# Attention products of two local-attention models: the order of row halves in two of them, and which operand is loaded in a third

## Chip, cores and metric

The kernel runs on one core of a Trainium2 chip. The metric is the device time of one execution in microseconds (us). The kernel before was run three times: 4997.42, 5001.14 and 5006.03 us, median 5001.14.

## What is computed

The input is x with 2 x 2048 rows of 128 features, all in float32. Four blocks follow each other, each behind a layer norm with a modulation and with a gated residual:

1. an attention in chunks of 64 rows with a running memory,
2. the **first model**: six layers of local attention (16 heads of 64, windows of 32 rows) and feed-forward,
3. a causal linear attention with feed-forward,
4. the **second model**: two layers of local attention (8 heads of 64, windows of 64 rows) and feed-forward.

The change touches only the local attention of the two models. Cut to what matters, one layer of it is:

```python
qkv = shift(x) @ Wqkv                      # W = 32, 16 heads; or W = 64, 8 heads
q, k, v = heads(qkv)                       # heads of 64 features
q, k = rotary(l2norm(q) * qs, l2norm(k) * ks)
# each window of W rows sees its own W keys and those of the window before
sim = einsum('bhwie,bhwje->bhwij', q * 8.0, look(k))     # 2W keys per row
sim = where(mask, -max, sim)
attn = softmax(sim)
out = einsum('bhwij,bhwje->bhwie', attn, look(v))
x = x + merge_heads(out) @ Wo
x = x + feed_forward(shift(x))
```

## The kernel before

The function `local_models` runs both models and the linear attention between them as one stream of tiles. A tile is 128 rows of one batch. A layer has 32 tiles (16 in each of two batches), so there are 6 x 32 = 192 tiles of the first model and 2 x 32 = 64 of the second. The main loop (line 1471) is a software pipeline: in one turn it works on the scores of tile i+1, on the projection of queries and keys of tile i+3 (`project`), on the values of tile i+2 (`values`), on the value product and the output of tile i (`mix`, `turn_out`, `project_out`). The work of the feed-forward and of the linear attention is put in between in steps. The order in which the program is written gives priorities; a planner then sets the final order of the instructions on each engine and gives out the buffers. [...] The activations lie with features on the partitions (`hs`), so that a tile of them can be the loaded operand of the projections.

The steps of a tile that matter here:

- `scores` (line 974): a mask is put into two banks of PSUM by two products (line 986), and the products of queries and keys are added to it. `q` counts the two halves of the rows of the operands: partitions 0 to 63 hold one head and partitions 64 to 127 another, since a head has 64 features. `w` counts the windows in a tile, NW = 4 in the first model and 2 in the second. `cc` counts pairs of heads, 8 and 4. So there are 64 products a tile in the first model (64 rows deep, 32 columns loaded, 64 moving) and 16 in the second (64 deep, 64 loaded, 128 moving). A product's output goes to the partitions of its window; its half q decides the bank.
- softmax over the scores: VectorE takes the maximum and subtracts it (1003, 1005), ScalarE the exponential (1012), VectorE the sums (1019), GpSimd the scaling (1021).
- `keys_first_` (line 1023): TensorE turns the weights so that the keys lie on the partitions, and ScalarE copies them into `pT` (1031), which has one buffer, shared with `oT`.
- `mix` (line 1034): the value product. `NO` is 2 in the first model and 1 in the second: 2W keys fill 64 or 128 partitions, so that in the first model the two halves `s` of the rows hold different heads, whose outputs go to two banks `po[s]`. In the first model there are 64 products of 64 x 32 loaded by 64 moving, in the second 16 of 128 x 64 by 64. The turned weights `pT` are loaded, the values `v2` move; the result has the tile's rows on the partitions. ScalarE copies it into `on` (1053).
- `turn_out` (line 1056): TensorE turns `on` (4 transposes for each of NO), ScalarE copies it into `oT` (1064).
- `turn` (line 923): TensorE turns queries and keys of tile i+2 (936).
- `project_out` (line 1067): the product of the output weights with `oT` (1075), added to the residual by VectorE (1081).

The profile counts each float32 product as two records, and each transpose as one.

Of the kernel before, what the change touches and what calls it, by code (L numbers as in the profile page):

```python
# [72 lines left out]
def tile_kernel(ctx: ExitStack, tc: tile.TileContext, a: dict, out: bass.AP):  # L73
    nc = tc.nc
# [26 lines left out]
    def bc(ap, shape):  # L101
        return ap.to_broadcast(list(shape))
# [605 lines left out]
    def local_models(mA, mB, hs0):  # L708
# [8 lines left out]
        def wide(name):  # L717

            return psA.tile([128, 1024], F32, tag="A", name=f"ps_{name}")

        def bank(name):
            return psT.tile([128, 512], F32, tag="T", name=f"ps_{name}")
# [53 lines left out]
        st = [dict() for _ in range(n)]  # L776
# [4 lines left out]
        def load_proj(g, u):  # L781

            m, l = layers[g]
            w = wpool.tile([128, 1024], F32, tag="wp", name="wp", bufs=4)
            c = u * 1024
            k = min(1024, 3 * m.INNER - c)
            nc.sync.dma_start(w[:, 0:k], a[f"{m.pre}_ffn_Wqkv"][l, :, c:c + k])
            wts[g, u] = w

        def load_out(g):  # L790
            m, l = layers[g]
            w = wpool.tile([128, 8, 128], F32, tag="wo", name="wo", bufs=2)
            nc.sync.dma_start(
                w[:, 0:m.NPR, :], a[f"{m.pre}_ffn_Wo"][l].rearrange("(c p) m -> p c m", p=128)
            )
            wts[g, "o"] = w
# [41 lines left out]
        def factors(g):  # L838
            m, l = layers[g]
            f = wk.tile([128, 2, 2, DH], F32, name="fac", bufs=2)  # L840
            nc.vector.scalar_tensor_tensor(
                f[:, 0], m.sc, RSQ_C, m.qsc[:, :, l, :], ALU.mult, ALU.mult
            )
            for lo in (0, 32):
                nc.vector.tensor_copy(f[:, 1, :, lo:lo + 32], f[:, 0, :, 32 - lo:64 - lo])
            fac[g] = f
# [127 lines left out]
        def scores(i):  # L974

            g, b, t = tiles[i]
            m, _ = layers[g]
            W, H, HPG = m.W, m.H, m.HPG
            qT, kT = st[i].pop("q"), st[i].pop("k")
            sp = wide("s")  # L980
            for q in range(2):


                rows, sel, j = (slice(0, 128), identb, 0) if t == 0 else (
                    slice(64 * q, 64 * q + 64), pick, 1)
                nc.tensor.matmul(
                    sp[:, 512 * q:512 * q + 512], lhsT=sel[rows],
                    rhs=bc(m.maskb[rows, j].unsqueeze(1), (rows.stop - rows.start, HPG, 2 * W)),
                    start=True, stop=False,
                )  # L990
            for cc in range(HPG):
                for q in range(2):
                    for w in range(m.NW):
                        c0 = 512 * q + 2 * W * cc
                        nc.tensor.matmul(  # L995
                            sp[W * w:W * w + W, c0:c0 + 2 * W],
                            lhsT=qT[64 * q:64 * q + 64, cc, W * w:W * w + W],
                            rhs=kT[64 * q:64 * q + 64, cc, W * w:W * w + 2 * W],
                            start=False, stop=(cc == HPG - 1),
                        )  # L1000
            v = lambda x: x.rearrange("p (h k) -> p h k", k=2 * W)
            mx = wk.tile([128, 16], F32, name="mx")
            nc.vector.tensor_reduce(mx[:, 0:H], v(sp), AX.X, ALU.max)  # L1003
            sm = wk.tile([128, 1024], F32, name="sm", bufs=2)
            nc.vector.tensor_tensor(
                v(sm), v(sp), bc(mx[:, 0:H].unsqueeze(2), (128, H, 2 * W)), ALU.subtract
            )
            st[i]["p"] = sm

        def weights_exp(i):  # L1010
            sm = st[i]["p"]
            nc.scalar.activation(sm, sm, AF.Exp)  # L1012

        def weights_norm(i):
            m, _ = layers[tiles[i][0]]
            sm = st[i]["p"]
            v = sm.rearrange("p (h k) -> p h k", k=2 * m.W)
            rs = wk.tile([128, 16], F32, name="rs", bufs=2)[:, 0:m.H]
            nc.vector.tensor_reduce(rs, v, AX.X, ALU.add)  # L1019
            nc.vector.reciprocal(rs, rs)  # L1020
            nc.gpsimd.tensor_tensor(v, v, bc(rs.unsqueeze(2), (128, m.H, 2 * m.W)), ALU.mult)  # L1021
# [12 lines left out]
        def mix(i):  # L1034

            m, _ = layers[tiles[i][0]]
            W, NO = m.W, m.NO
            pT, v2 = st[i].pop("pT"), st[i].pop("v")
            po = [bank("o") for _ in range(NO)]
            on = wk.tile([128, 2, 4, 128], F32, name="on")  # L1040
            for c in range(4):
                for s in range(NO):
                    kp = slice(2 * W * s, 2 * W * (s + 1))
                    for q in range(2):
                        co = 128 * c + 64 * q
                        for w in range(m.NW):
                            nc.tensor.matmul(  # L1047
                                po[s][W * w:W * w + W, co:co + 64],
                                lhsT=pT[kp, q, c, W * w:W * w + W],
                                rhs=v2[kp, w, co:co + 64], start=True, stop=True,  # L1050
                            )
            for s in range(NO):
                nc.scalar.copy(on[:, s].rearrange("p c i -> p (c i)"), po[s])  # L1053
            st[i]["on"] = on
# [34 lines left out]
        def step():  # L1089
            if steps:  # L1090
                steps.pop(0)()
# [4 lines left out]
        def lstep():  # L1096
            if lsteps:
                lsteps.pop(0)()
# [372 lines left out]
        for i in range(-3, n):  # L1471
            j = i + 3
            lstep()
            if 0 <= i + 1 < n:
                scores(i + 1)
                weights_exp(i + 1)
                weights_norm(i + 1)
            more = False
            if j < n:
                g, b, t = tiles[j]  # L1480
                jj = j % per
                nu = len(layers[g][0].units)
                more = g < last
                if g == second and t % 4 == 0:
                    while (b, t // 4) not in ready:
                        lstep()
                if nu == 2:
                    project(j, 0)
                if more and jj == 4:
                    load_proj(g + 1, 0)  # L1490
                if more and jj == 6 and g + 1 == second:
                    models[1].consts()
                if jj == 6 and g == second - 1:
                    linear_consts()
                if more and jj == 8:
                    factors(g + 1)
                    if 2 == 2:
                        load_out(g + 1)
                if more and jj == 18:
                    load_ff(g + 1)  # L1500
                if more and jj == 22:
                    fold_ff(g + 1)
                if nu == 2 and more and jj == per - 1:
                    load_proj(g + 1, 1)
                lstep()
            step()
            if i >= 0:
                keys_first_(i)
            if 0 <= i + 2 < n:
                halo(i + 2)  # L1510
            if j < n:
                project(j, nu - 1)
                if nu == 2 and more and jj == per - 1 and g + 1 < second:
                    load_proj(g + 1, 2)
                if nu == 1 and more and jj == per - 1:
                    load_proj(g + 1, 1)
                if b == B - 1 and j + 1 < n:
                    tables(*tiles[j + 1][::2])
            lstep()
            if i >= 0:  # L1520
                mix(i)
            lstep()
            if 0 <= i + 2 < n:
                values(i + 2)
            lstep()
            if i >= 0:
                turn_out(i)
            if 0 <= i + 2 < n:
                for u in range(len(layers[tiles[i + 2][0]][0].units)):
                    turn(i + 2, u)  # L1530
            step()
            lstep()
            if i >= 0:
                g, b, t = tiles[i]
                project_out(i)
                if 2 == 1 and i % per == per - 1 and g < last:
                    load_out(g + 1)
                if t % 4 == 3:
                    feed_forward(g, b, t // 4)
# [9 lines left out]
    with ExitStack() as ctx2:  # L1549
        local_models(m0, m1, hs0)  # L1550
# [63 lines left out]
```

## Time and profile before

| | |
|---|---|
| runs, median | 5001.14 us |
| profiled execution, own time | 5004.26 us |
| its span | 5002.5 us |
| granted TensorE clock, mean | 0.961 |
| TensorE, matmuls busy | 4572.7 us (91%) |
| TensorE, weight loads busy | 3143.2 us (63%) |
| VectorE busy | 3973.1 us (79%) |
| ScalarE busy | 2883.5 us (58%) |
| GpSimd busy | 2780.8 us (56%) |
| chain of waits | TensorE 53%, VectorE 20%, ScalarE 8%, GpSimd 5% |

The span divides into the first block, up to about 641 us, the first model, from there to about 4050 us (with the first steps of the linear attention in its last layer), and the second model, to the end. Busy time is the time in which at least one instruction of the group was under way, so that overlapping records count once; it is smaller than the count times the mean. A line of a group reads: line, engine, operation, output and inputs by name, shapes and count, then busy us and mean ns of one, then the idle time of the engine just before these instructions and what ended most of it. For TensorE, 64\*32 is the loaded operand's depth and columns, and 64x64 the moving operand.

### The profile page before, as it was taken

The numbers are of one execution on the slowest core, as the hardware profiler recorded it, in microseconds if no ns is written. First come the engines' busy times: TensorE is split into PE (matmuls) and PEld (weight loads), VectorE is DVE, ScalarE is ACT, GpSimd is POOL, SyncE is SP. The second block draws the span as 40 slices with busy tenths as digits, with TensorE's granted clock in tenths as the row PEclk, the third lists the DMA queues.
The fourth block names the chain that finished last, engine by engine and source line by source line (L and its number), as shares of the span: only waits on it lengthen the run. The fifth ranks groups of instructions, "written<-read, shape, count | busy, mean of one in ns | idle before, by whom it ended". The sixth has DMA issues, their size and how long they took to land.

```text
span 5002.5 us, 170719 instructions
## 1 busy us (share of the span) xinstructions
PE 4572.7 (91%) x74820; PEld 3143.2 (63%) x74850; DVE 3973.1 (79%) x6840; ACT 2883.5 (58%) x4665; POOL 2780.8 (56%) x1666
## 2 busy tenths in 40 slices
PE   5667799999999999999999999999999989899897
PEld 4445566666666666666666666666666666555554
DVE  6993488888888888888888888888877777787885
ACT  3233366666666656666666666666555555565564
POOL 3332366666666666666666666666555544455452
PEclk8778899999999999999999999999999999999999
DMA  2000322222222322223222322232222211111111
GB/s 77 1 1 25 84 69 67 63 72 74 71 64 63 83 71 63 63 76 76 66 66 64 83 67 64 65 78 73 54 55 52 63 45 38 39 46 40 53 53 37
DMA packets 222487, 295.59 MB, mean 59 GB/s; under 512 B 75656, under 2 KB 95408, under 8 KB 221744
## 3 DMA queue, kind: packets, MB, share of 16 engines
q1 hardware_dynamic: 221744, 284.67, 22.0%
q8 instruction: 590, 9.67, 0.8%
q14 instruction: 153, 1.25, 0.1%
HBM read 40.98 MB, written 10.75 MB: 10 GB/s over the span
## 4 chain that ended last, share of the span: by engine, by line
PE 53%; DVE 20%; ACT 8%; POOL 5%; issue 3%; DMA 1%; SPq 0%; POOLq 0%; ACTq 0%; DVEq 0%
PE ps_qk L871 11%; PE ps_v L955 6%; PE ps_f L1158 5%; PE ps_turn L936 5%; PE ps_y L1075 5%; PE ps_o L1047 5%; PE ps_s L995 4%; DVE ps_qk L897 4%; POOL r L892 3%; DVE t L886 3%; PE ps_fy L1183 3%; PE ps_oT L1063 3%; ACT sq L873 2%; DVE r L881 2%; PE ps_pT L1030 2%
## 5 line engine op out<-in xcount | busy, mean ns | idle before, releaser
L892 POOL TENSOR_TENSOR r<-r,t 128x1024 f32<-128x1024 f32 x448 | 1061.2, 2369 | 995.9 <-DVE t L886 770.5
L904 POOL TENSOR_TENSOR r<-r,rq_y 128x1024 f32<-128x1024 f32 x448 | 844.0, 1902 | 455.9 <-DVE rq_y L180 439.2
L873 ACT ACTIVATE sq<-ps_qk 128x1024 f32<-128x1024 f32 x448 | 460.4, 1028 | 1006.4 <-PE ps_qk L871 999.9
L871 PE MATMUL ps_qk<-wp,hs 128*128 128x512 f32 x1792 | 884.4, 615 | 68.3 <-DVE rq_y L180 41.3
L881 DVE TENSOR_TENSOR r<-ps_qk,tb 128x1024 f32<-128x1024 f32 (+1 forms) x512 | 550.1, 1074 | 175.4 <-ACT sq L873 166.9
L886 DVE TENSOR_TENSOR t<-ps_qk,tb 128x1024 f32<-128x1024 f32 (+1 forms) x512 | 553.2, 1080 | 145.0 <-POOL r L892 144.5
L1021 POOL TENSOR_TENSOR sm<-sm,rs 128x1024 f32<-128x1024 f32 x256 | 487.2, 1903 | 263.3 <-DVE rs L1020 172.3
L897 DVE TENSOR_REDUCE ps_qk<-sq 128x16 f32<-128x1024 f32 x448 | 549.1, 1226 | 12.3
L1047 PEld LDWEIGHTS ps_o<-v,pT 64*32 64x32 f32 (+1 forms) x26624 | 356.8, 109 | 289.1 <-ACT pT L1031 175.7
L871 PEld LDWEIGHTS ps_qk<-wp,hs 128*128 128x128 f32 x1792 | 306.7, 191 | 326.2 <-issue 235.6
L955 PE MATMUL ps_v<-wp,hs 128*128 128x512 f32 x896 | 471.9, 639 | 1.0 <-ACT on L1053 0.6
L1047 PE MATMUL ps_o<-v,pT 64*32 64x64 f32 (+1 forms) x26624 | 418.1, 224 | 59.6 <-ACT pT L1031 32.7
L1075 PEld LDWEIGHTS ps_y<-oT,wo 128*128 128x128 f32 x3584 | 429.2, 192 | 48.0 <-issue 42.2
L936 PE MATMUL ps_turn<-ident,r 128*128 128x128 f32 x3584 | 443.2, 276 | 13.3 <-POOL r L904 11.8
L1075 PE MATMUL ps_y<-oT,wo 128*128 128x128 f32 x3584 | 446.3, 276 | 1.8 <-ACT oT L1064 1.8
L936 PEld LDWEIGHTS ps_turn<-ident,r 128*128 128x128 f32 x3584 | 405.7, 143 | 19.8 <-POOL r L904 16.6
L1003 DVE TENSOR_REDUCE mx<-ps_s 128x16 f32<-128x1024 f32 (+1 forms) x256 | 312.9, 1222 | 110.8 <-PE ps_s L995 107.4
L995 PE MATMUL ps_s<-kT,qT 64*32 64x64 f32 (+1 forms) x26624 | 371.6, 230 | 0.4
L1019 DVE TENSOR_REDUCE rs<-sm 128x16 f32<-128x1024 f32 (+1 forms) x256 | 310.3, 1212 | 68.6 <-ACT sm L1012 67.5
L1158 PE MATMUL ps_f<-fx,w 128*128 128x512 f32 (+1 forms) x768 | 356.4, 600 | 1.7 <-DVE fx L1141 1.7
L995 PEld LDWEIGHTS ps_s<-kT,qT 64*32 64x32 f32 (+1 forms) x26624 | 321.3, 107 | 57.1 <-issue 46.2
L956 ACT COPY vn<-ps_v 128x512 f32<-128x512 f32 x448 | 262.5, 586 | 112.3 <-PE ps_v L955 93.4
(268 smaller groups left out, 7554.6 us busy)
## 6 DMA issues: line engine op xcount, KB each, us to landing
v<-vn SPq DMA_DIRECT2D x1276, 128.0 KB
v<-vn SPq DMA_DIRECT2D x744, 64.0 KB
v<-vn SPq DMA_DIRECT2D x64, 256.0 KB
wp<-in_L_ffn_Wqkv SPq DMA_DIRECT2D x20, 512.0 KB
xD<-xb SPq DMA_DIRECT2D x24, 256.0 KB
xb<-xD SPq DMA_DIRECT2D x24, 256.0 KB
cs<-in_cos SPq DMA_DIRECT2D x128, 32.0 KB
cs<-in_sin SPq DMA_DIRECT2D x128, 32.0 KB
```

The costliest lines, as they stand in the source:

```text
L871: nc.tensor.matmul(pq[:, js], lhsT=hw, rhs=wts[g, u][:, js], start=True, stop=True)
L881: nc.vector.tensor_tensor(r[:, es].rearrange("p (h d) -> p h d", d=DH), pq[:, es].rearrange("p (h d) -> p h d", d=DH), bc(tb[:, 0, s].unsq ...
L886: nc.vector.tensor_tensor(t2[:, es].rearrange("p (h s d) -> p h s d", s=2, d=32), pq[:, es].rearrange("p (h s d) -> p h s d", s=2, d=32)[: ...
L892: nc.gpsimd.tensor_tensor(r, r, t2, ALU.add)
L897: nc.vector.tensor_reduce(pq[:, 16 * v:16 * v + 16], st[i].pop(("sq", v)).rearrange("p (h d) -> p h d", d=DH), AX.X, ALU.add,)
L904: nc.gpsimd.tensor_tensor(rv, rv, bc(y[:, 16 * v:16 * v + 16].unsqueeze(2), (128, 16, DH)), ALU.mult)
L936: nc.tensor.transpose(p[:, c * 128:(c + 1) * 128], r[:, cs], ident)
L955: nc.tensor.matmul(p, lhsT=hw, rhs=wv, start=True, stop=True)
L995: nc.tensor.matmul(sp[W * w:W * w + W, c0:c0 + 2 * W], lhsT=qT[64 * q:64 * q + 64, cc, W * w:W * w + W], rhs=kT[64 * q:64 * q + 64, cc, W ...
L1047: nc.tensor.matmul(po[s][W * w:W * w + W, co:co + 64], lhsT=pT[kp, q, c, W * w:W * w + W], rhs=v2[kp, w, co:co + 64], start=True, stop=True,)
L1075: nc.tensor.matmul(py[:, 0:128], lhsT=wts[g, "o"][:, c * NO + s, :], rhs=oT[:, s, c, :], start=(c + s == 0), stop=(c == 3 and s == NO - 1),)
L1158: nc.tensor.matmul(ps_[c][0:sz], lhsT=wts[g, "w1"][:, o:o + sz], rhs=S["x"], start=True, stop=True,)
```

## The change

There are three edits.

1. In `scores` the loops over w and q change places: the products go from one half of the rows to the other at each product, where before one half had NW products in a row. This applies to both models.
2. In `mix` for the first model the loop over s goes from second to innermost: the two halves s alternate at each product, where before one half had eight products in a row.
3. In `mix` for the second model the operands change places: `v2` is the loaded operand and `pT` moves. The result has the features on the partitions, as `project_out` needs it, so it is copied once into `on` and goes to `project_out` from there. `turn_out` is left out for tiles of the second model.

```diff
             for cc in range(HPG):
-                for q in range(2):
-                    for w in range(m.NW):
+                for w in range(m.NW):
+                    for q in range(2):
                         c0 = 512 * q + 2 * W * cc
...
             on = wk.tile([128, 2, 4, 128], F32, name="on")
+            if NO == 1:
+
+                for c in range(4):
+                    for w in range(m.NW):
+                        for q in range(2):
+                            co = 128 * c + 64 * q
+                            nc.tensor.matmul(
+                                po[0][64 * q:64 * q + 64, 128 * c + W * w:128 * c + W * w + W],
+                                lhsT=v2[:, w, co:co + 64], rhs=pT[:, q, c, W * w:W * w + W],
+                                start=True, stop=True,
+                            )
+                nc.scalar.copy(on[:, 0].rearrange("p c i -> p (c i)"), po[0])
+                st[i]["o"] = on
+                return
             for c in range(4):
-                for s in range(NO):
-                    kp = slice(2 * W * s, 2 * W * (s + 1))
-                    for q in range(2):
-                        co = 128 * c + 64 * q
-                        for w in range(m.NW):
+                for q in range(2):
+                    co = 128 * c + 64 * q
+                    for w in range(m.NW):
+                        for s in range(NO):
+                            kp = slice(2 * W * s, 2 * W * (s + 1))
                             nc.tensor.matmul(
...
-            if i >= 0:
+            if i >= 0 and "on" in st[i]:
                 turn_out(i)
```

## The prediction

> **What bounds the kernel now.** I read the table of stretches first, then the groups by shape of TensorE, then single blocks in the timeline, and last the waits of the second model.
>
> Columns of the first fence: the stretch, then busy time (and records) of PE, PEld, DVE, ACT and POOL, the granted clock, DMA share, GB/s. The first row is one layer of the first model, 32 tiles; the second is most of the second model.
>
> ```profile
> 1735.00:2289.00 554.00, 539.03 (x10430) 374.47 (x10432) 463.34 (x741) 349.08 (x560) 354.25 (x206) 0.99 0.28 69
> 4562.00:5002.00 440.00, 380.89 (x3324) 242.25 (x3320) 331.38 (x679) 243.81 (x368) 196.94 (x121) 0.96 0.17 46
> ```
>
> In a layer of the first model TensorE is busy 539 of 554 us, VectorE 463 (84%). A microsecond taken from TensorE there comes off the end nearly whole, until VectorE is next. In the second model TensorE has 381 of 440 (87%), VectorE 75%: no engine is full, and waits count too.
>
> ```profile
> L1047 PE MATMUL ps_o<-v,pT 64*32 64x64 f32 x24448 | 324.5, 223 | 36.2 <-issue 26.0 <-ACT pT L1031 9.2
> L995 PE MATMUL ps_s<-kT,qT 64*32 64x64 f32 x24192 | 292.3, 225 | 0.4
> ...
> L1063 PE MATMUL ps_oT<-ident,on 128*128 128x128 f32 x1532 | 201.7, 275 | 2.3 <-ACT on L1053 2.3
> ```
>
> These are the first model (641 to 4050 us). The two small-product groups have the same 64 products (128 records) for each of 192 tiles. Per tile the scores take 292.3/192 = 1.52 us and the value product 324.5/192 = 1.69 us: 0.17 us more for the same count of the same size.
>
> The stretches inside one scores block (first two rows, line L995) and one value block (last two, L1047) show where. Every window is 0.24 us long; a record counts if it overlaps the window.
>
> ```profile
> 2256.87:2257.11 0.24, 0.24 (x32) 0.24 (x33) 1.00 0.28 68
> 2257.80:2258.04 0.24, 0.24 (x44) 0.24 (x27) 1.00 0.86 188
> ...
> 2316.24:2316.48 0.24, 0.24 (x25) 0.24 (x29) 1.00 0.00 0
> 2317.20:2317.44 0.24, 0.24 (x44) 0.24 (x35) 1.00 0.00 0
> ```
>
> The first window starts with nothing in flight: scores 32 records in 0.24 us, 7.5 ns each; values 25, 9.6 ns each. Later records last some 0.22 us, so 44 overlapping ones mean 44/(0.24+0.22) = 96 a microsecond, 10.5 ns each, the same in both. So the blocks differ in their opening, where work stands ready; afterwards both go at one pace, which I read as the pace of issue.
>
> In the second model:
>
> ```profile
> L1063 PE MATMUL ps_oT<-ident,on 128*128 128x128 f32 x252 | 42.4, 293 | 27.8 <-ACT on L1053 27.3
> L1064 ACT COPY oT<-ps_oT 128x512 f32<-128x512 f32 x63 | 37.0, 588 | 36.8 <-PE ps_oT L1063 36.8
> L1053 ACT COPY on<-ps_o 128x512 f32<-128x512 f32 x63 | 36.7, 582 | 25.9 <-PE ps_o L1047 25.7
> ```
>
> The turning of the output costs TensorE 42.4 us busy and 27.8 us idle, waiting for the copy of `on`. One tile of it, in the timeline of TensorE:
>
> ```profile
> 4588.18 1.04 PE L1047 MATMUL ps_o<-v,pT 128*64 128x64 f32 x28
> 4589.90 0.66 PE L1063 MATMUL ps_oT<-ident,on 128*128 128x128 f32 x4 [0.68 <-ACT on L1053]
> 4590.39 1.04 PE L936 MATMUL ps_turn<-ident,r 128*128 128x128 f32 x8
> ```
>
> The value product is over, TensorE stands 0.68 us, and the turns of `r` that are queued behind stand too.
>
> [...]
>
> **The change part by part.**
>
> *Scores, 192 tiles (and 64 of the second model).* Same instructions; TensorE's order outside the block is the same in the first model but for its first steady tile. The old order runs four products on one row half, then four on the other, so all eight tiles of the array come round once in eight products; the new order also visits each once in eight. As nothing in the opening or the pace of issue should change, I take 0. Bounds: if everything ran at the opening's 7.5 ns, a block would take 128 x 7.5 ns + 0.23 us = 1.19 us, 0.33 less, 63 us in all; a loss is treated as a rival. In the second model the order goes from row half outermost to strip outermost over four tiles, whose 32 records take 1.10 us: 0.
>
> *First model's value product, 192 tiles.* Here the old order has eight products in a row on one row half: each of the four tiles gets two products before the other half is touched. Alternating gives it the scores' pattern, so I expect the scores' time at best: 0.17 x 192 = 32 us. Part of the 0.17 is not order: in some tiles the block is cut by a value projection (L955) and pays its tail, one record of 0.22 us, and a restart a second time. Such cuts number some 40 by the timeline; at about 0.3 us they make 12 us. So 20 us, bounds 0 and 0.50 x 192 = 96 us (1.69 to 1.19). All on the path, TensorE being 97% busy.
>
> *Second model's value product, 64 tiles.* 16 products with the 64 columns of V as loaded operand and 64 token columns moving; before 64 token columns loaded and 64 of V moving. Shape 128x64 by 128x64 either way, the two column strips alternate either way: 0. The result already has the features on the partitions.
>
> *Removed: turning the output, 64 tiles.* Four transposes and one ScalarE copy a tile: on TensorE 42.4 us busy, and up to 27.8 us of standing. On ScalarE 37.0 us, which is busy 244 of 440 us there and so has room: 0 by themselves. The lower bound is the 2.8% that the chain of waits from 4050 to 5002 us gives to `ps_oT`: 0.028 x 952 = 27 us. The upper is 42.4 + 27.8 = 70 us. TensorE is busy 87% here, and part of the standing will come back as waits for VectorE, whose max and subtraction have 4.6% and 4.9% of that chain. I take 48.
>
> *What is late next.* `project_out` now waits for the copy of `on` itself. Between the value product and it, TensorE has the eight turns of `r` (1.04 us) and mostly a value projection (1.13 us); the copy takes 0.58 us. Covered; without cover it would be 0.6 x 64 = 38 us. Behind that wait stand the next tile's mask and score products. The single buffer of `on` is now held until `project_out` has read it, which precedes the next value product on TensorE: no wait. The buffer shared by `pT` and `oT` is freed after the value product instead of after `project_out`: the copy of the next `pT` can go earlier, which I leave at 0, as it is queued on ScalarE behind others.
>
> *The planner's order in the second model* changes on all engines: VectorE and GpSimd swap neighbours (scaling of `r` and of `sm`), and SP issues its fetches and stores of x in other places among the value copies. SP's DMA share there is 0.17, so these stay hidden. I take 0, between -15 and +15 us.
>
> *Sum.* 20 + 48 = 68 us. The profiled execution ran 5004.26 us (span 5002.5 and 1.8 around it), so 4936; the median of the runs shown, 5001.14, is 3 lower. 4935 allows for part of that.
>
> **Rivals.**
> 1. *Alternation speeds the whole block* (both blocks at 7.5 ns throughout): 63 + 96 + 48 = 207 us, about 4795. For it: the opening shows that the array can. Against: the scores already change halves every four products and yet fall to 10.5 ns. Chance 0.08.
> 2. *The turning was in the shadow*: the freed 42.4 us of the second model are eaten by VectorE's chain (subtraction and max lead it), less than 15 remain: 5001 - 20 - 10 = about 4971 to 4981. For it: 13% idle on TensorE. Against: TensorE itself stood for 27.8 us there. Chance 0.13.
> 3. *Slower: two halves in one column strip exclude each other.* In the new order neighbours sit in the same strip. The opening's eight tiles at 7.5 ns mean about 8 x 7.5 = 60 ns for one record on its tile; if only four strips work, 128/4 x 60 ns + 0.23 = 2.15 us a block, +0.63 for scores and +0.46 for values, 209 us in all, less 48: about 5160; half of it, about 5060. It decides from 48/192 = 0.25 us per tile. Against it stands the first stage, whose scores already alternate halves in one strip:
>
> ```profile
> 445.58 1.09 PE L411 MATMUL ps_s<-kx,qT 64*64 64x512 f32 x8
> ```
>
> Eight records of 512 columns in 1.09 us, while two such full-height records of `ps_v` alone take 1.13: the four tiles run together. Chance 0.07.
>
> That the change doesn't do what it says is out: four transposes a tile are gone from TensorE's order.
>
> **How the numbers follow.** Main case 0.72, at 4935; its own range is 4880 to 4968 (20 may be 0 to 60, 48 is 27 to 70). With the second rival the range becomes 4882 to 4983 and leaves out the first and third, 0.15. A measurement here tells 0.2%, 10 us, from no change. Faster by more than that: 0.72 + 0.08 + nearly all of 0.13, 0.91; within: 0.02; slower: 0.07.
>
> **What would show it.** L995 64*32 near 292 us and the value product's row near 305; no `ps_oT` rows after 4050 and no idle time of `ps_y` for the copy of `on`; a layer of the first model 3 us shorter, the second model some 45. Wrong if score blocks change by more than 0.1 us either way, or if the second model keeps its length.

## The result: slower by half a per cent, and the profile after

Five runs of the changed kernel and five of the kernel before on the same chip gave medians of 5023.68 us (5021.63 to 5036.48) and 5006.03 us (4997.42 to 5007.68). The ratio is 1.0047, with a 95% interval from 1.0033 to 1.0061: slower by 17 to 31 us. The forecast was 66 us faster. The profiled execution took 5036.48 us (span 5034.7), the longest of the five.

From the first residual addition of each layer (L1081 before, L1095 after) the time divides so:

| us | before | after |
|---|---|---|
| to the first residual of the first model | 641.5 | 649.2 |
| first model, six layers | 3408.9 | 3432.1 |
| second model, to the end | 952.0 | 953.4 |

The first row holds nothing that was changed, and in the profiles below it lies between 635 and 650 us, so that two single profiles can differ by 7 us a stage, or some more, without cause. The first model lost 23 us, and the second gained nothing. Both gains of the forecast are missing, so there are two questions.

The stretches that the prediction began with, in the changed kernel (its first row lies some 17 us earlier in the work):

```profile
1735.00:2289.00 554.00, 534.24 (x10430) 369.52 (x10430) 463.55 (x744) 348.46 (x561) 354.00 (x207) 0.99 0.28 69
4562.00:5002.00 440.00, 380.98 (x3413) 246.17 (x3412) 340.19 (x711) 230.07 (x347) 217.66 (x133) 0.95 0.17 48
```

TensorE is busy 534 us where it was 539, for the same number of records: it has less to do in a layer, and takes as long. In the second model it is busy 381 of 440 us, as before.

**First model.** The two groups, in the groups by shape of TensorE over the first model of the changed kernel. L1061 is the value product, L1047 before.

```profile
L1061 PE MATMUL ps_o<-v,pT 64*32 64x64 f32 x24448 | 306.9, 226 | 64.4 <-issue 53.1 <-ACT pT L1031 10.3
L995 PE MATMUL ps_s<-kT,qT 64*32 64x64 f32 x24384 | 294.3, 226 | 0.7 <-issue 0.5
```

The busy time did what was forecast: 306.9 us where 305 was written, and the scores are at 12.1 ns a record as before (294.3/24384; 292.3/24192). In the blocks without a gap the 32nd record starts 0.26 us after the first (0.33 before) and the 128th 1.27 us (1.36 before), in the middle of all such blocks: most of the gain lies in the opening, as was argued. The last part of the row is what matters. TensorE stands 64.4 us ahead of records of this group (36.2 before), and 53.1 us of it (26.0 before) carry the name "issue", for which the profile shows no releaser. A busy row that falls by 17.6 us beside an idle entry that grows by 28.2 us is a loss, though only of 11 of the 23 us.

One tile shows where. This is TensorE's timeline around the value product of the fifteenth tile, first of the kernel before, then of the changed one (start, length, line, records, and in brackets the idle time ahead).

```profile
861.96 1.02 PE L871 MATMUL ps_qk<-wp,hs 128*128 128x512 f32 x2
862.92 1.80 PE L1047 MATMUL ps_o<-v,pT 64*32 64x64 f32 x128
864.65 1.12 PE L955 MATMUL ps_v<-wp,hs 128*128 128x512 f32 x2
```

```profile
872.92 1.50 PE L1061 MATMUL ps_o<-v,pT 64*32 64x64 f32 x107
876.51 0.42 PE L1061 MATMUL ps_o<-v,pT 64*32 64x64 f32 x21 [2.09 <-issue]
876.86 0.70 PE L955 MATMUL ps_v<-wp,hs 128*128 128x512 f32 x1
```

After 107 of its 128 records the block stands for 2.09 us, though all of its operands were there: the 21 records behind the gap use the same `pT` and `v2`. The stretches of 0.5 us in the same tile (busy time and records of PE, granted clock, DMA share, GB/s) show what happens meanwhile:

```profile
872.92:873.42 0.50, 0.46 (x30) 1.00 0.00 0
873.42:873.92 0.50, 0.50 (x64) 1.00 0.16 33
873.92:874.42 0.50, 0.50 (x54) 1.00 0.00 0
874.42:874.92 0.50, 0.00 (x1) 1.00 0.00 0
...
876.42:876.92 0.50, 0.41 (x22) 1.00 0.00 0
```

33 GB/s over 0.5 us are 16 KB: one transfer, in the middle of the block. It belongs to the queue that the page calls instruction:

```profile
q8 instruction: 588, 9.63, 0.8%
```

9.63 MB in 588 packets are 16 KB each. TensorE's part of this trace has 150632 records, counting matmuls, weight loads and the semaphore instructions of its queue: 256 for each packet. So I counted these records through the trace. Every one of the changed kernel's 35 gaps of over 0.6 us inside a value block lies at the same place of the count, 163 modulo 256 give or take one, and so do all 16 of the kernel before. (Without the semaphore instructions the places scatter.) In each of the 35 the first record behind the gap follows 1.2 to 1.6 us after the end of the transfer of a packet. From this I read the gap as TensorE waiting for its next packet of instructions. These gaps make 28.5 us before and 60.7 us after. In the fifteenth tile, counted from the previous edge:

| us after the previous edge | before | after |
|---|---|---|
| next packet begins | 0.86 | 5.79 |
| value block begins | 4.83 | 4.84 |
| block reaches the packet's end | 6.17 | 6.12 |
| first record of the next packet | 6.18 | 8.42 |

After, the first record of the next packet follows 2.63 us behind the packet's beginning. Before, the packet began at once and had 5.3 us; after, it began 4.9 us later, only when the block was already running.

**Second model.** First the turning of queries and keys in the groups of the kernel before from 4050 to 5002 us, then the groups of the changed kernel from 4081 to 5034 us. L1089 is `project_out`, L1172 the hidden layer of the feed-forward (L1158 before).

```profile
L936 PE MATMUL ps_turn<-ident,r 128*128 128x128 f32 x488 | 67.8, 285 | 8.3 <-POOL r L904 8.3
```

```profile
L936 PE MATMUL ps_turn<-ident,r 128*128 128x128 f32 x488 | 73.8, 297 | 32.8 <-POOL r L904 32.8
L1089 PE MATMUL ps_y<-on,wo 128*128 128x128 f32 x507 | 72.8, 290 | 1.5 <-ACT on L1052 1.5
L1172 PE MATMUL ps_f<-fx,w 128*128 128x512 f32 x144 | 81.4, 693 | 2.1 <-DVE fx L1155 1.8
```

No row of `ps_oT` is left, and `project_out` waits 1.5 us in all for the copy of `on`: that cover held. But the turning of `r` (L936) now waits 32.8 us for GpSimd's scaling of `r` (L904), 8.3 before.

### The profile page after: what moved, and what is told of

Read it like the earlier page. It is cut to its first block, busy times and chain, and to the rows that moved or that the text cites. A ratio compares the mean times of both kernels' runs of the same rounds, so it can differ in the third digit from the quotient of the medians.

```text
span 5034.7 us, 170087 instructions
## 1 busy us (share of the span) xinstructions
PE 4557.0 (91%) x74564; PEld 3122.2 (62%) x74594; DVE 3968.2 (79%) x6840; ACT 2840.4 (56%) x4591; POOL 2784.4 (55%) x1666
## 3 DMA queue, kind: packets, MB, share of 16 engines
q8 instruction: 588, 9.63, 0.8%
## 4 chain that ended last, share of the span: by engine, by line
PE 54%; DVE 19%; ACT 7%; POOL 5%; issue 3%; DMA 1%; SPq 0%; POOLq 0%; DVEq 0%; ACTq 0%
PE ps_qk L871 12%; PE ps_v L955 6%; PE ps_turn L936 5%; PE ps_f L1172 5%; PE ps_y L1089 5%; PE ps_s L995 4%; PE ps_o L1061 4%; DVE ps_qk L897 4%; DVE t L886 4%; POOL r L892 3%; PE ps_fy L1197 3%; DVE r L881 2%; PE ps_oT L1077 2%; PE ps_pT L1030 2%; ACT sq L873 2%
## 5 line engine op out<-in xcount | busy, mean ns | idle before, releaser
L904 POOL TENSOR_TENSOR r<-r,rq_y 128x1024 f32<-128x1024 f32 x448 | 844.6, 1903 | 443.6 <-DVE rq_y L180 427.0
L936 PE MATMUL ps_turn<-ident,r 128*128 128x128 f32 x3584 | 451.1, 278 | 41.3 <-POOL r L904 36.3
L936 PEld LDWEIGHTS ps_turn<-ident,r 128*128 128x128 f32 x3584 | 407.9, 144 | 61.1 <-POOL r L904 43.2
L1061 PEld LDWEIGHTS ps_o<-v,pT 64*32 64x32 f32 x24576 | 262.9, 105 | 226.0 <-ACT pT L1031 138.8
L1089 PEld LDWEIGHTS ps_y<-oT,wo 128*128 128x128 f32 x3072 | 363.5, 192 | 33.4 <-issue 32.2
L1089 PE MATMUL ps_y<-oT,wo 128*128 128x128 f32 x3072 | 375.0, 275 | 0.1
L1061 PE MATMUL ps_o<-v,pT 64*32 64x64 f32 x24576 | 309.2, 226 | 64.6 <-issue 53.1
L1172 PE MATMUL ps_f<-fx,w 128*128 128x512 f32 (+1 forms) x768 | 364.6, 612 | 2.1 <-DVE fx L1155 1.8
L1031 ACT COPY pT<-ps_pT 128x512 f32<-128x512 f32 x512 | 274.0, 585 | 101.6 <-PE ps_pT L1030 101.1
```

The costliest lines, as they stand in the source:

```text
L904: nc.gpsimd.tensor_tensor(rv, rv, bc(y[:, 16 * v:16 * v + 16].unsqueeze(2), (128, 16, DH)), ALU.mult)
L936: nc.tensor.transpose(p[:, c * 128:(c + 1) * 128], r[:, cs], ident)
L1061: nc.tensor.matmul(po[s][W * w:W * w + W, co:co + 64], lhsT=pT[kp, q, c, W * w:W * w + W], rhs=v2[kp, w, co:co + 64], start=True, stop=True,)
L1089: nc.tensor.matmul(py[:, 0:128], lhsT=wts[g, "o"][:, c * NO + s, :], rhs=oT[:, s, c, :], start=(c + s == 0), stop=(c == 3 and s == NO - 1),)
L1172: nc.tensor.matmul(ps_[c][0:sz], lhsT=wts[g, "w1"][:, o:o + sz], rhs=S["x"], start=True, stop=True,)
```

## Experiments

Two theories went in. A: in the first model the new order of the value product makes the next packet of instructions come late; in the second the freed time became waits for GpSimd. The rivals were that the scores do the harm, that a faster block runs out of instructions whatever its order, and that VectorE's chain sets the second model's pace. In what follows "gaps" are those of over 0.6 us between the starts of two matmul records of one value block of the first model, with no other matmul between them; the expectations' 31 and 62 us are an earlier, slightly wider count of the 28.5 and 60.7 us above. "Saved" and "lost" are the ratio times 5004 us.

| run | ratio to before, 95% | gaps, us | first model | second model |
|---|---|---|---|---|
| before | 1 | 16, 28.5 | 3408.9 | 952.0 |
| changed kernel | 1.0047 (1.0033 to 1.0061) | 35, 60.7 | 3432.1 | 953.4 |
| e1_second | 0.9997 (0.9983 to 1.0011) | 11, 20.0 | 3404.0 | 951.0 |
| e2_values | 1.0030 (1.0019 to 1.0041) | 32, 51.9 | 3426.0 | 949.1 |
| e3_scores | 0.9994 (0.9983 to 1.0006) | 20, 35.2 | 3414.8 | 943.6 |
| e4_old_open | 0.9996 (0.9982 to 1.0009) | 14, 25.2 | 3402.0 | 948.7 |
| e5_touch | 1.0035 (1.0022 to 1.0049) | 2, 2.1 | 3428.2 | 949.9 |
| e6_touch_old | 1.0049 (1.0035 to 1.0062) | 2, 1.3 | 3433.0 | 954.8 |
| e8_turn_late | 0.9910 (0.9896 to 0.9925) | 20, 34.7 | 3417.9 | 913.6 |
| e9_all_touch_late | 0.9944 (0.9930 to 0.9958) | 0, 0 | 3423.6 | 919.4 |
| e10_one_touch | 0.9885 (0.9865 to 0.9905) | 7, 6.8 | 3385.7 | 918.1 |
| e11_late_open | 0.9909 (0.9891 to 0.9926) | 15, 23.9 | 3400.5 | 912.9 |
| e12_shift | 1.0078 (1.0056 to 1.0099) | 34, 62.6 | 3442.7 | 952.7 |
| e13_late_only | 0.9972 (0.9963 to 0.9981) | 16, 28.5 | 3402.9 | 935.2 |

The columns of stages are from one profile each, the ratios from all runs.

### Which edit costs

Each edit was put alone into the kernel before, as in the diff of the change.

*Edit 1, the scores:*

> Edit 1 alone: in the scores of both models the halves alternate at each product; the order on every engine is otherwise that of the kernel before. Theory A (the loss is not in the scores): 0, within 8 us of before either way, the row of ps_s 64*32 within 2 us of 292. Rival B (scores delay the packets for the value block that follows): 10 to 25 us slower, gaps within the value block up by 20 us or more.

Measured 0.9994 (0.9983 to 1.0006): no difference that can be told. The scores don't cause the loss.

*Edit 2, the value product of the first model:*

> Edit 2 alone: in the first model's value product the halves alternate at each product. Theory A (late instruction packets): the block's busy time falls by some 18 us, and gaps within it of over 0.6 us, all at one place of every 256 records of TensorE, rise from about 31 us to about 62 us in all; first model 10 to 25 us longer, the whole 10 to 25 us slower. Rival B (the scores' new order did it): first model some 18 us shorter, the whole 10 to 20 us faster.

Measured 15 us lost (10 to 21), and 32 gaps of 51.9 us. This edit alone makes the first model slower. The changed kernel lost 24 us (17 to 31); the intervals overlap, and whether the other 9 us have a cause of their own stays open.

*Edit 3, the second model:*

> Edit 3 alone on the kernel before: only the second model's value product has its operands exchanged and its turning is gone; the orders of edits 1 and 2 stay old. Theory A (the time that the removed turning gave TensorE came back as waits for GpSimd's scaling of r): second model as long as before, 945 to 958 us, rows ps_oT gone there, some 25 to 35 us of idle time of ps_turn for POOL r; the whole 0 to 10 us from the kernel before. Rival B (the second model's edit gains, and what the first model lost hid it): second model 25 to 50 us shorter, the whole 25 to 50 us faster.

Measured 0.9997, and a second model of 951.0 us: removing 252 transposes with 70 us of busy and idle time gained nothing that can be told (some 8 us at most, by the interval). The timeline shows what came instead, first TensorE, then GpSimd.

```profile
4703.96 0.39 PE L986 MATMUL ps_s<-L_maskb,pick 64*128 64x512 bf16 x2 [0.33 <-DVE rq_y L180]
4707.60 1.97 PE L936 MATMUL ps_turn<-ident,r 128*128 128x128 f32 x8 [3.25 <-POOL r L904]
4709.36 1.92 PE L1172 MATMUL ps_f<-fx,w 128*128 128x512 f32 x2
```

```profile
4703.79 1.90 POOL L1021 TENSOR_TENSOR sm<-sm,rs 128x1024 f32<-128x1024 f32 x1 [4.63 <-DVE ps_qk L178]
4705.65 1.90 POOL L904 TENSOR_TENSOR r<-r,rq_y 128x1024 f32<-128x1024 f32 x1
```

GpSimd takes the weights `sm` first and then `r`, 1.90 us each, and TensorE stands for `r` all that time. It stands so before eleven turnings, and ahead of ten of them GpSimd had this order. In the trace's order of GpSimd the weights come ahead of the `r` of the same round in 10 rounds of the second model; in the kernel before they do in 3. The order is the planner's, and it is new in both kernels that leave the transposes and copies out. Then TensorE comes back at half its pace: the eight turns take 1.97 us here, where they took 1.04 in the prediction's timeline. The stretches around this wait show the granted clock at half (stretch, then busy time and records of PE, PEld, DVE, ACT and POOL, granted clock, DMA share, GB/s):

```profile
4700.00:4704.00 4.00, 3.15 (x36) 1.72 (x34) 3.73 (x11) 2.52 (x4) 0.21 (x1) 1.00 0.00 0
4707.50:4709.40 1.90, 1.80 (x9) 1.80 (x10) 1.66 (x9) 0.59 (x1) 1.90 (x2) 0.50 0.03 9
```

In the trace's record of the clock it is at half from 4706.0 to 4712.8 us, 5.2 us beyond the end of the wait (4707.60). In all the second model has 98 us at half clock in this run, 111 in the changed kernel and 73 in the kernel before.

### Why the packet comes late

In the new order the second half of the rows is first touched by the second product of a tile, and that product waits for two transfers (the two pieces of the first window of `v2`), often for the bank too. In the old order it is the fifth product or, in most tiles, the ninth; the planner decides which. (In the fifteenth tile of the traces the wait for semaphore 103, one that transfers raise, stands at the second product after and at the fifth before.) The kernel before thus holds its own experiment. Blocks that another product cuts in two (26 of 192) are left out. Of the others, 47 before have the edge of a packet behind the 96th record or later:

| where the second product with several waits stands before | tiles | with a gap over 0.6 us | the same tiles in the changed kernel, where it is the second |
|---|---|---|---|
| ninth | 30 | 2 | 19 |
| fifth | 17 | 12 | 14 |

That suggested that the packet comes late where a product with several waits stands near the opening of the block. It is a reading of these counts: how such a wait would hold up a packet, and what sets off a packet's transfer, no run shows. Of the 17 tiles five begin 41 to 45 records behind an edge, all with the wait in the fifth place; in two of them (the fifteenth tile is one) the packet began 0.9 us after the edge, in three 6 to 7 us after it. One run kept the old order for the first 16 of the 64 products:

```diff
-                for s, q, w in (new order):
+                for s, q, w in ((old order) if c == 0 else (new order)):
```

> Edit 2, but the first 16 of a tile's 64 value products keep the old order, so that the second half of the rows is first touched at the fifth or ninth product as before; the other 48 alternate. Theory A ([...] in the new order that is the second product, so the next instruction packet is asked for too late): gaps over 0.6 us in the block back near 31 us in all, busy time of the block still 10 to 18 us lower, the whole 5 to 20 us faster than before. Rival B (a block that goes faster runs out of instructions, wherever the waits stand): gaps some 50 to 60 us, the whole 5 to 25 us slower, like edit 2 alone.

The gaps went back to 14 of 25.2 us, with the block's busy time from 660 to 4030 us still 12 us below before (311.0 and 322.9). The whole is at 0.9996: the loss of edit 2 is gone, but the gain of 5 to 20 us that was expected did not show. The rival, that a fast block runs dry wherever its waits stand, falls.

Two more runs took the waits away from the block instead of moving them. A small product that reads the first window of `v2` is written ahead of the transposes of the weights, into the bank that these then overwrite:

```diff
                 p = bank("pT")
+                if (first model):
+                    kp = slice(64 * q, 64 * q + 64)
+                    nc.tensor.matmul(p[0:32, 0:32], lhsT=v2[kp, 0, 0:32], rhs=v2[kp, 0, 0:32],
+                                     start=True, stop=True)
                 for c in range(4):
```

> Edit 2 with two small extra products a tile of the first model (64 x 32 loaded, 32 moving), written ahead of the turning of the weights: they read the values' first window and so take the waits for its transfers beforehand, and no value product has to wait for more than one semaphore; what they write is overwritten. Theory A [...]: gaps of over 0.6 us in the block fall from some 52 us with edit 2 alone to below 15 us, busy time stays about 18 us under before, the extra products cost 0 to 12 us, the whole 15 to 45 us faster than before. Rival B (a fast block runs out of instructions, wherever the waits stand): gaps 30 to 60 us, the whole 0 to 25 us slower.

> The kernel before with the same two extra products a tile, the value product in its old order. Theory A: gaps of over 0.6 us in the block fall from 28 us to below 15 us, the whole 5 to 25 us faster. Rival B: gaps stay at 20 to 35 us, the whole 0 to 12 us slower for the extra products.

The gaps all but vanished in both, 2.1 and 1.3 us. The edges of the packets did not leave the blocks: 43 uncut blocks still have one behind the 96th record or later, and 2 of these have a gap. Yet both kernels are slower, by 18 and 24 us. The groups by shape from 660 to 4030 us, first the value product before, then two rows of the first of the two runs, and that run's timeline in the fifteenth tile, say why:

```profile
L1047 PE MATMUL ps_o<-v,pT 64*32 64x64 f32 x24320 | 322.9, 223 | 36.2 <-issue 26.0 <-ACT pT L1031 9.2
```

```profile
L1052 PE MATMUL ps_o<-v,pT 64*32 64x64 f32 x24064 | 287.9, 226 | 6.1 <-ACT pT L1038 3.5 <-issue 2.4
L1037 PE MATMUL ps_pT<-ident,sm 128*128 128x128 f32 x1504 | 247.7, 287 | 0.0
```

```profile
866.00 0.24 PE L1031 MATMUL ps_pT<-v 64*32 64x32 f32 x2
866.18 0.66 PE L1037 MATMUL ps_pT<-ident,sm 128*128 128x128 f32 x4
866.76 0.25 PE L1031 MATMUL ps_pT<-v 64*32 64x32 f32 x2
866.94 0.66 PE L1037 MATMUL ps_pT<-ident,sm 128*128 128x128 f32 x4
867.43 1.88 PE L871 MATMUL ps_qk<-wp,hs 128*128 128x512 f32 x4
```

The value product stands only 6.1 us now and is busy 287.9, but from the first small product to the next projection 1.43 us pass. In the kernel before the eight transposes of this tile take 0.91 us:

```profile
860.12 1.04 PE L1030 MATMUL ps_pT<-ident,sm 128*128 128x128 f32 x8
861.03 1.95 PE L871 MATMUL ps_qk<-wp,hs 128*128 128x512 f32 x4
```

From the first of these records to the next of another kind, the tiles from 660 to 3390 us take 1.43 us on average, and 0.96 in the kernel before: 0.47 us a tile or 90 us in all 192, more than the 65 us that the block gave back (36.2 to 6.1 idle, 322.9 to 287.9 busy). The two small products of another tile shape are dear here: those 90 us are an estimate from the 0.47 us, and the expectations had allowed 12.

The last run on this question leaves everything as changed and only shifts the edges, by 128 records:

```diff
+        p = bank("pad")
+        for k in range(32):
+            nc.tensor.matmul(p[:, 0:128], lhsT=ident, rhs=ident, start=True, stop=True)
```

> The changed kernel with 32 extra float32 products, 128 records and so half a packet of instructions, once at the start of the two models; the order is otherwise the same but for a handful of places. Theory A (the gaps stand at the edges of instruction packets): the edges move by 64 products records within every tile, tiles that had gaps have none, others have them; in all 40 to 80 us of gaps, the whole within 15 us of the changed kernel, at 0 to 35 us slower than before. Rival B (the gaps belong to certain tiles, through the clock or a transfer): the same tiles have gaps.

```profile
867.83 0.59 PE L874 MATMUL ps_qk<-wp,hs 128*128 128x512 f32 x1
868.35 1.73 PE L1062 MATMUL ps_o<-v,pT 64*32 64x64 f32 x128
870.01 1.12 PE L958 MATMUL ps_v<-wp,hs 128*128 128x512 f32 x2
```

The fifteenth tile runs through. There are 34 gaps of 62.6 us, all again at 163 or 164 modulo 256 of the count, and not one is in a tile that had one in the changed kernel. So the gaps belong to the edges of packets, not to certain tiles, through the clock or another transfer. By the ratios the whole was 39 us slower than before, where 35 had been the most expected, and 16 above the changed kernel; the intervals overlap (1.0056 to 1.0099 and 1.0033 to 1.0061). The added products explain some 8 us, by an estimate from `project_out`'s records of the same shape in the kernel before (446.3 us busy for 3584, so 0.125 us for each of the 64 matmul records added); the rest stays open.

### Whether the second model's gain can be set free

In the run with edit 3 alone the turning of `r` was written after `project_out` for the second model. Nothing else is different, but the planner now keeps `r` ahead of the weights on GpSimd in all but one round of the trace.

```diff
-            if 0 <= i + 2 < n:
+            late = i >= 0 and (second model)
+            if 0 <= i + 2 < n and not late:
                 for u in range(...):
                     turn(i + 2, u)
...
                 project_out(i)
+                if 0 <= i + 2 < n and late:
+                    for u in range(...):
+                        turn(i + 2, u)
```

> Edit 3 alone, with the turning of r in the second model written after project_out; in the planner's order GpSimd then scales r ahead of the weights in all but 2 of the tiles (12 with edit 3 alone, 1 to 3 before). Theory A (the freed time went into TensorE waiting for r, which GpSimd scales 1.9 us later where the weights come first): idle time of ps_turn for POOL r in the second model falls from 32.8 us to below 15 us, the second model 15 to 40 us shorter, the whole 15 to 40 us faster than before. Rival B (VectorE's chain sets the second model's pace): another wait takes its place, second model 940 to 958 us, the whole within 8 us of before.

The groups of this run in the second model:

```profile
L936 PE MATMUL ps_turn<-ident,r 128*128 128x128 f32 x491 | 65.8, 274 | 1.2 <-POOL r L904 0.9 <-DVE ps_qk L167 0.2
L1089 PE MATMUL ps_y<-on,wo 128*128 128x128 f32 x504 | 72.3, 286 | 10.8 <-ACT on L1052 10.1
```

The wait for `r` is gone (0.9 us), `project_out` pays 10.1 us for the lost cover, and the second model takes 913.6 us: 45 us saved in all (38 to 52), slightly more than the 40 allowed. The rival, that VectorE's chain would take the time, falls. Whether the later place of the turning on TensorE or the order on GpSimd did more was not told apart. How much of it is edit 3's? The late turning was put into the kernel before without it:

> The kernel before with the late turning of r in the second model alone, no other edit. Theory A (before, TensorE waited for r only some 8 us there, and the gain of edit 3 is set free by the late turning, not made by it): 0 to 12 us faster than before. Rival B (the order alone brings it): 30 to 50 us faster, second model 905 to 925 us.

It saves 14 us (9 to 19), slightly more than theory A allowed, and its second model takes 935.2 us. Taken with edit 3 the late turning is worth 37 us of the second model (951.0 to 913.6), without it 17; edit 3 is worth 22 us with the late turning (935.2 to 913.6) and 1 without.

Much of this goes with the granted clock. In the second model the clock stood at half for 73 us before, 98 in e1_second, 67 in e8_turn_late and 44 in e13_late_only. As a rough estimate, count half of that time as lost. The five runs whose second model has the same program (before, e2, e4, e5, e6) took 948.7 to 954.8 us with 62 to 76 us at half clock; without the lost half all five come to 915 to 918 us, so the estimate fits. By it, edit 3 alone is worth 13 us and gives 12 of them back as half clock; the late turning alone is worth 2 us, and 14 of its 17 are clock; edit 3 beside the late turning is worth 33 us, not 22. No run changed the clock by itself.

### Kernels that beat both

> All three edits, with the extra products and with the late turning of r. Theory A: the two gains add, 35 to 80 us faster than before. Rival B (one of the two has no effect): no faster than the better of the two kernels that have it alone, 0 to 30 us faster.

All three edits with both extra products and the late turning: 28 us saved (21 to 35), where 35 to 80 were expected. The late turning gives its 45, and the extra products take some 18 back, as in e5_touch; not the sum that was expected.

> All three edits, the first 16 value products of a tile in the old order, the turning of r written late, no extra products. Theory A (the gains of the two runs that had these parts alone add): gaps in the value block 20 to 40 us, the second model 912 to 925 us, the whole 40 to 60 us faster than before. Rival B (the late turning gains only beside the old first model): 0 to 35 us faster.

All three edits, the first 16 products in the old order, the late turning: 46 us saved (37 to 55). The additions to e8_turn_late, edit 1 and the mixed order, bring nothing that can be measured, as they did alone.

```diff
-                if (first model):
-                    nc.tensor.matmul(p[0:32, 0:32], lhsT=v2[kp, 0, 0:32], rhs=v2[kp, 0, 0:32], ...)
+                if q == 0 and (first model):
+                    nc.tensor.matmul(p[:, 0:1], lhsT=ident, rhs=v2[:, 0, 0:1], start=True, stop=True)
```

> As the run with all three edits, the extra products and the late turning, but with one extra product a tile of the first model in place of two: the identity loaded over the full height, one column of the values moving, of the same shape of tile as the transposes that follow. Theory A (the two extra products of another tile shape cost some 0.24 us a tile, 45 us in all, and ate what the vanished gaps gave): gaps in the value block stay below 10 us in all, row of ps_pT some 15 to 25 us over the 203 us it has without extra products rather than 45, the whole 45 to 65 us faster than before. Rival B (not their shape, but the early wait for the values' transfers costs the 45 us): still 20 to 35 us faster only.

One extra product a tile, of the transposes' own shape, in place of two. 58 us saved (48 to 68), the best of all. By the same measure the transposes with it take 1.10 us a tile, 0.13 more than before in place of 0.47. That there is one product in place of two, and that its shape is another, were not told apart. In the groups by shape:

```profile
L1064 PE MATMUL ps_o<-v,pT 64*32 64x64 f32 x24320 | 299.0, 226 | 14.0 <-issue 8.7 <-ACT pT L1036 3.0
L1035 PE MATMUL ps_pT<-ident,sm 128*128 128x128 f32 x1528 | 210.5, 278 | 1.8 <-ACT u L1185 1.8
```

The first model takes 3385.7 us, 23 less than before and 46 less than in the changed kernel. Some 10 of the 23 can be put down to the clock, by the same estimate (44 us at half clock in this stage, 65 before). How much of the rest is edit 2's was not measured: no run has the single extra product with the old order.

## Why the prediction was wrong, step by step

- *Scores, 0*: right (edit 1 alone 0.9994).
- *First model's value product, -20 us*: the busy time fell by 17.6 us, most of it in the opening, so the argument on the order and its size were right. (The cuts by a value projection that it counted as some 40 are 25 in the trace.) The sentence that failed is "All on the path, TensorE being 97% busy". It counts busy time alone. The row that the prediction itself printed had "issue 26.0" in its idle part, and that term was put at nothing: the only "issue" in the prediction is a pace of 10.5 ns a record. Most of that entry was whole gaps of 0.7 to 2.5 us at the edges of packets, and the new order doubled them (28.5 to 60.7 us). In place of -20 stood +15 (edit 2 alone), outside the bounds of 0 and 96 faster.
- *Second model's value product as such, 0*: near enough; busy 90.1 to 93.5 us.
- *Removed turning, -48 us, bounds 27 to 70*: measured about 1 alone (0.9997). The busy and idle time of `ps_oT` did go. The step that failed is "The planner's order in the second model ... I take 0, between -15 and +15 us": it named the swap of GpSimd's two scalings, and left it unpriced, though each is 1.90 us and a queued turn of `r` waits for the second of them. With edit 3 alone TensorE had eleven waits of 1.9 to 3.5 us for `r` (32.8 us in all, 8.3 before). Its busy time in the second model fell by 15 us only, from 841.0 to 825.9, and some 9 of the missing 27 go, by the estimate above, with the longer half clock (83 of the busy us at half clock, 65 before, half of the difference). Even with the order mended the term was too large as measured: 22 us of the second model, below its lower bound. Beside the transposes' 42.8 us, the other products' rows grew there (the value product from 81.6 to 90.6, the hidden layer from 75.1 to 80.9), so that TensorE's busy time fell by only 13.6 us, from 833.2 to 819.6. About 11 us of the growth are, by the same estimate, again the clock (59 busy us at half clock in place of 36); the rest stays open.
- *What is late next*: `project_out` was covered, 1.5 us. But the question was asked only of what depends on the removed step, not of what stands ahead of the next instruction on TensorE, the turning of `r`.
- *Rivals*: the second, "the turning was in the shadow", described what happened in the second model, with a wrong agent: GpSimd's order in place of VectorE's chain. The third, slower through halves that exclude each other, had the right sign for a wrong reason: the busy time fell. A rival for the unexplained "issue" was missing. The range of the main case, 4880 to 4968 us, is narrower than its own bounds give (4871 to 4974 from 5001); the measured time lies outside both.

## What to carry to other kernels

An idle entry that the profile gives to "issue" is not a pace until its gaps have been looked at one by one: count the engine's records, its semaphore instructions among them, and see if the long gaps stand at one place modulo 256, as all 35 of the changed kernel did. Where a dense block of small products begins with products that wait for several transfers, try them in later places (e4_old_open: gaps of 25.2 us in place of 51.9), or take these waits ahead of the block, and compare the shapes of the instruction that does it: the single one of full height cost 0.13 us a tile, the two of 64 x 32 cost 0.47. Where a planner sets the order, a removed step is priced only when the new order of every engine has been read for what now stands ahead of the next wait; a swap of two operations of 1.9 us on an engine that is busy 55% of the span (2784.4 of 5034.7 us) hid what the late turning then set free. And look at the granted clock beside the idle time: in e1_second it was still at half for 5.2 us after a wait of 3.25 us had ended.

## What was not expected of the hardware

- At a late packet of instructions TensorE stood for up to 2.6 us in the changed kernel and 2.5 us before, from one record's start to the next, and in the value blocks of the kernel before, the changed kernel and e12_shift only where the edge falls on the 96th to 128th record of a block of 128 matmuls (256 records with the weight loads). Half of all packets begin no later than 0.9 us after the previous edge, in the kernel before and in the changed one.
- Moving the second product with several waits from the ninth or fifth place to the second, with no more than that and the alternation changed, took the gaps from 28.5 us to 51.9 (e2_values); with the first 16 products in the old order they were 25.2 (e4_old_open). That it is the number of waits, and not the transfers that they wait for, was not told apart: the extra products took both away (2.1 us in e5_touch).
- In e1_second, after a stand of 3.25 us, eight transposes took 1.97 us, and the two 512-column records behind them 1.92; in the kernel before the eight took 1.04 us. The granted clock had gone to half 1.6 us into the stand and stayed there for 6.8 us.
- Two products of 64 x 32, each ahead of a group of 128 x 128 transposes, cost 0.47 us a tile (e5_touch: 1.43 us, 0.96 before); one of full height with a single column moving, 0.13 us (e10_one_touch: 1.10).
